# Selective scan: decays of the GpSimd steps in SBUF, exponentials and b emitted up to three steps ahead

## The chip, the core and the metric

The kernel runs on one NeuronCore of a Trainium2 chip. The core has TensorE (PE, matrix products into PSUM), VectorE (DVE), ScalarE (ACT, activation functions), GpSimd (POOL) and a queue engine SyncE (SP) that issues transfers. Each engine takes its instructions in the order in which they were put in its queue; semaphores make one engine wait for another. The metric is the device time in microseconds (us) of one execution. The kernel before takes 29,334.67 us, the median of three runs (29,313.72 to 29,365.72).

## The reference

Sixteen images of 48 x 48 positions and 96 channels go through two layers. Each layer normalises, projects to 192 channels, applies a 3 x 3 depthwise convolution and SiLU, and then runs a selective scan in four directions (row-wise and column-wise, forward and backward). After the scan come a gate, an output projection and a feed-forward block in rounded number formats; layer 0 also has a convolutional branch. Nearly all of the time goes to the scan. Cut to what matters, for each channel d, state n (16 of them) and direction:

```python
h = h * exp(delta_t * A[d, n]) + (delta_t * u_t) * B_t[n]
y_t = sum over n of h[d, n] * C_t[n]      # then + D * u_t
```

It runs over L = 2304 positions. The factor exp(delta A) is the decay; the second term is called b below.

## The kernel before, in words

**Tiles.** A scan works on tiles of 128 partitions by CH = 768 positions, in float32. The 128 partitions hold 32 channels times 4 states. One image and layer needs two passes ("pair" 0 forward, 1 backward), each over NCH = 3 chunks of 768 positions, 3 groups j of 128 channels, 4 blocks i of 32 channels, and GROUPS = 4 groups g of states: STEPS = 288 steps. There are 32 scans (16 images, 2 layers), so 9216 steps.

**One step.** In `scan`, a step n makes, in this order of the program:

1. `loaded` (L461) asks for `d` (delta and delta x u of 32 channels, repeated for 4 states; 4 buffers) when g is 0, and for `bc` (B and C of 4 states, repeated for 32 channels; 6 buffers) when these change. Both are issued on SyncE.
2. `begun` (L481) calls it, then makes the decay `a` with an exponential on ScalarE (L484) into PSUM, in one of two buffers of the pool `ps`, and the product `b` on GpSimd (L486) into one of four SBUF buffers.
3. The recurrence itself is one scan instruction on VectorE (L518): h = a h + b along 768 positions, started from the `carry` column of the chunk before.
4. The product `hc` = h x C (L520; 4 buffers).
5. ScalarE copies the last column of h into `carry` (L522).
6. TensorE multiplies `hc` with the 0/1 matrix `fold_sb` (L524) and adds it up in `py`, over the 16 steps of one j; then ScalarE copies `py` out (L533). The first addend of `py` is the skip term or the y of the forward pass, loaded as `first` (L502) and added at L504.

**Who makes hc.** `SHARE = (1, 0, 0, 0)` and the line

```python
here = SHARE[self.turn % len(SHARE)] == 0
```

split the steps. Of each four, one (g = 0) has its product made by GpSimd. [...]there the scan writes h to an SBUF tile `h` (two buffers). In the other three the scan overwrites the decay in PSUM and VectorE makes the product from there.

**Order.** Before step n's scan, the program has written down the exponential and b of step n + 1 (`ready` holds them). The program's order is not yet that of the queues: the framework's scheduler places each engine's instructions from that order and from the buffers that it expects to be free.

**Other work.** `together` runs the scan of one image beside the remaining work of its neighbours (`first`, `middle`, `final`: normalisation, convolutions, projections, gate, feed-forward). That work is a generator which is advanced in proportion to the steps done, so a given part of it always stands beside the same steps. It uses its own buffers, and all five engines.

Of the kernel before, what the change touches and what calls it, by code (L numbers as in the profile page):

```python
# [11 lines left out]
F32 = mybir.dt.float32  # L12
# [3 lines left out]
AF = mybir.ActivationFunctionType  # L16
ALU = mybir.AluOpType
# [13 lines left out]
CH = 2 * SUB  # L31
# [5 lines left out]
SHARE = (1, 0, 0, 0)  # L37
# [82 lines left out]
def sub(ap):  # L120
    return ap.rearrange("p (q f) -> p q f", f=SUB)
# [16 lines left out]
class Net:  # L138
    def __init__(self, ctx, tc, wpack, at, b2, ffw):
        self.tc, self.nc = tc, tc.nc  # L140
        nc = self.nc
# [31 lines left out]
        for t in ("l0", "l1"):  # L173
            a = self.const.tile([128, 2 * 12 * GROUPS], F32, name=t + "_a")
# [3 lines left out]
            d = self.small.tile([128, 3], F32, name="dsum")  # L178
# [8 lines left out]
        for t, bias in (("bn1", "e1b"), ("bn2", "e2b")):  # L187
# [4 lines left out]
            b = self.const.tile([128, 3], F32, name=t + "_b")  # L192
# [7 lines left out]
        for v, name in (("g", "ong"), ("b", "onb")):  # L200
            for i, half in enumerate("ab"):
                n = (128, 64)[i]
# [25 lines left out]
        for name, w, at in (  # L228
# [11 lines left out]
            d = self.dram.tile([128, 9 * 128], F32, name="taps_" + name)  # L240
# [5 lines left out]
        for i in range(2):  # L246
            d = lambda name, shape: self.dram.tile(shape, F32, name=f"{name}_{i}")
# [7 lines left out]
                    "dd": {(p, j): d(f"dd{p}{j}", [128, NCH * 2 * CH]) for p in range(2) for j in range(3)},  # L255
                }
            )
        self.turn = 0

    def get(self, name):  # L260
        at, width, rows = self.at[name]
# [186 lines left out]
    def scan(self, t, s):  # L448

        nc = self.nc  # L450
        rates = self.a[t].rearrange("p (a b i g) -> p a b i g", a=2, b=3, i=4)
        steps = []
        for pair in range(2):
            for c in range(NCH) if pair == 0 else reversed(range(NCH)):
                for j in range(3):
                    for i in range(4):
                        for g in range(GROUPS):
                            steps.append((pair, c, j, i, g))
        held = {}

        def loaded(pair, c, j, i, g):  # L461

            if g == 0:
                d = self.sw.tile([128, 2, CH], F32, name="d", bufs=4)
                rows = s["dd"][pair, j][32 * i : 32 * i + 32, c * 2 * CH : (c + 1) * 2 * CH]
                nc.sync.dma_start(
                    d.rearrange("p w f -> p (w f)"), rows.unsqueeze(1).broadcast_to([ND, NG, 2 * CH])
                )
                held["d"] = d
            kk = KK[j][32 * i]  # L470
            if (j, i) in ((0, 0), (1, 2)):
                b = self.sw.tile([128, 2, CH], F32, name="bc", bufs=6)
                at = (2 * pair + kk) * NS + g * NG
                rows = s["bc"][at : at + NG, c * 2 * CH : (c + 1) * 2 * CH]
                nc.sync.dma_start(
                    b.rearrange("p w f -> p (w f)"), rows.unsqueeze(0).broadcast_to([ND, NG, 2 * CH])
                )
                held["bc", g] = b
            return held["d"], held["bc", g]

        def begun(pair, c, j, i, g):  # L481
            d, bc = loaded(pair, c, j, i, g)
            a = self.ps.tile([128, 2, 512], F32, name="a", tag="ps").rearrange("p q f -> p (q f)")[:, :CH]
            nc.scalar.activation(a, d[:, 0, :], AF.Exp, scale=rates[:, pair, j, i, g : g + 1])  # L484
            b = self.sw.tile([128, CH], F32, name="b", bufs=4)
            nc.gpsimd.tensor_tensor(b, d[:, 1, :], bc[:, 0, :], ALU.mult)  # L486
            return a, b, bc[:, 1, :]

        ready = [begun(*steps[0])]
        before = carry = py = None  # L490
        for n, (pair, c, j, i, g) in enumerate(steps):
            if n + 1 < len(steps):
                ready.append(begun(*steps[n + 1]))
            a, b, cc = ready.pop(0)
            cs = slice(c * CH, (c + 1) * CH)
            if (j, i, g) == (0, 0, 0):
                before = carry if c != (0, NCH - 1)[pair] else None
                carry = self.sw.tile([128, 12 * GROUPS], F32, name="carry")
            if (i, g) == (0, 0):
                py = self.psy.tile([128, 2, 512], F32, name="py")  # L500
                first = self.sw.tile([128, CH], F32, name="first", bufs=1)
                nc.sync.dma_start(first, s["u" if pair == 0 else "y"][j][:, cs])  # L502
                for q in range(2):
                    nc.tensor.matmul(  # L504
                        py[:, q, :SUB],
                        lhsT=self.skip[t][:, j, :] if pair == 0 else self.ident,
                        rhs=first[:, q * SUB : (q + 1) * SUB],
                        start=True,
                        stop=False,
                    )  # L510
            way = (lambda ap: ap) if pair == 0 else (lambda ap: ap[:, ::-1])
            last = CH - 1 if pair == 0 else 0
            at = (4 * j + i) * GROUPS + g
            start = 0.0 if before is None else before[:, at : at + 1]
            here = SHARE[self.turn % len(SHARE)] == 0
            self.turn += 1
            h = a if here else self.sw.tile([128, CH], F32, name="h")
            nc.vector.tensor_tensor_scan(way(h), way(a), way(b), start, ALU.mult, ALU.add)  # L518
            hc = self.sw.tile([128, CH], F32, name="hc", bufs=4)
            (nc.vector if here else nc.gpsimd).tensor_tensor(hc, h, cc, ALU.mult)  # L520
            if c != (NCH - 1, 0)[pair]:
                nc.scalar.copy(carry[:, at : at + 1], h[:, last : last + 1])  # L522
            for q in range(2):
                nc.tensor.matmul(  # L524
                    py[:, q, :SUB],
                    lhsT=self.fold[:, i, :],
                    rhs=hc[:, q * SUB : (q + 1) * SUB],
                    start=False,
                    stop=((i, g) == (3, GROUPS - 1)),
                )  # L530
            if (i, g) == (3, GROUPS - 1):
                yt = self.sw.tile([128, CH], F32, name="yt", bufs=1)
                nc.scalar.copy(sub(yt), py[:, :, :SUB])  # L533
                nc.scalar.dma_start(s["y"][j][:, cs], yt)
            yield
# [245 lines left out]
def together(scan, others):  # L781


    total = sum(WORK[name] for name, _ in others)

    def all_others():
        for _, gen in others:
            yield from gen

    other, done = all_others(), 0  # L790
    for n, _ in enumerate(scan):
        while done < total * (n + 1) / (AHEAD * STEPS):
            done += next(other, 1e9)
    for _ in other:
        pass


@with_exitstack
def metaformer_kernel(ctx: ExitStack, tc: tile.TileContext, x, wpack, at, b2, ffw, fold, out):

    nc = tc.nc
    net = Net(ctx, tc, wpack, at, b2, ffw)
    net.fold = net.const.tile([128, 4, 128], F32, name="fold_sb")
    nc.scalar.dma_start(net.fold.rearrange("p a b -> p (a b)"), fold)
    image = lambda ap, m: ap[m].rearrange("(s p) c -> p s c", p=128)
    first = lambda m: ("first", net.first(m % 2, image(x, m)))
    middle = lambda m: ("middle", net.middle(m % 2, image(x, m)))
    final = lambda m: ("final", net.final(m % 2, image(out, m)))
    scan = lambda t, m: net.scan(t, net.s[m % 2])

    for _ in first(0)[1]:
        pass
    for m in range(0, NB, 2):
        together(scan("l0", m), [final(m - 1), first(m + 1)] if m else [first(m + 1)])
        together(scan("l0", m + 1), [middle(m)])
        together(scan("l1", m), [middle(m + 1)])
        together(scan("l1", m + 1), [final(m), first(m + 2)] if m + 2 < NB else [final(m)])
    for _ in final(NB - 1)[1]:
        pass
# [83 lines left out]
```

## Time and profile before

| What | Value |
|---|---|
| median of three runs | 29,334.67 us |
| the profiled execution | 29,326.56 us |
| its span, first to last instruction | 29,324.8 us |
| mean granted TensorE clock | 0.898 |
| busy: PE / VectorE / ScalarE / GpSimd | 82% / 80% / 48% / 79% |
| transfers | 4,406 MB, 150 GB/s, transfer engines 42% busy |

The profile describes one execution. Each group of instructions has its line, engine and operation, the tiles written and read (out<-in) with their shapes, the count, the total busy time, the mean duration in ns, and the idle time of the engine just before the instructions with what ended it ("<-"). A line of the view of waits reads: engine and tile that waited, "<-", what it waited for; then us in total, how many times, and the longest. Busy PE time is modelled from the ends of matmuls. The view by stretches gives the busy time of each engine in a stretch of the span, with the number of instructions in brackets, and behind them the TensorE clock, the busy share of the transfer engines and GB/s.

### The profile page before, as it was taken

What the parts mean: (1) busy time and instruction counts of PE and PEld (TensorE: products, weight loads), DVE (VectorE), ACT (ScalarE), POOL (GpSimd) and SP (SyncE); (2) the same over time, 40 slices, a digit from 0 to 9 for tenths busy, and PEclk for the clock granted to TensorE, in tenths of its full rate; (3) what the DMA queues carried; (4) which work ended last, traced back from release to release, by engine and by line L of the source; (5) the groups of instructions that cost most, each with busy time, mean ns of one, the idle gap of its engine ahead of it and who ended that gap; (6) DMA issues with size and microseconds to landing.
All of it is one profiled execution on the core that took longest, in us unless ns stands there. A gap on an engine that the chain in (4) does not pass through costs nothing. (4 is left out here: it accounts for less than half of the span.)

```text
span 29324.8 us, 227106 instructions
## 1 busy us (share of the span) xinstructions
PE 24033.6 (82%) x68224; PEld 12726.8 (43%) x68224; DVE 23488.3 (80%) x18372; ACT 14074.7 (48%) x22093; POOL 23241.6 (79%) x13238
## 2 busy tenths in 40 slices
PE   7888878888788887888788887888778888788886
PEld 3444444444444444444444444444444444344443
DVE  6877888778887788877888778887788877888777
ACT  4454444544445454444444444444444444444443
POOL 6877788778887788877888778787787877877777
PEclk8988899989999899998999989999898998989988
DMA  4444444444444444444444444444444344443443
GB/s 155 153 156 152 146 148 155 154 151 149 148 152 154 154 152 148 148 156 149 159 143 151 151 149 160 144 148 153 150 164 145 141 154 150 162 148 143 150 156 109
DMA packets 1062581, 4406.37 MB, mean 150 GB/s; under 512 B 211936, under 2 KB 211936, under 8 KB 1030368
## 3 DMA queue, kind: packets, MB, share of 16 engines
q1 hardware_dynamic: 869792, 3757.78, 36.2%
q10 hardware_dynamic: 191552, 634.06, 5.5%
q8 instruction: 536, 8.78, 0.1%
q14 instruction: 701, 5.74, 0.1%
HBM read 3500.22 MB, written 891.22 MB: 150 GB/s over the span
## 5 line engine op out<-in xcount | busy, mean ns | idle before, releaser
L486 POOL TENSOR_TENSOR b<-d,bc 128x768 f32<-128x768 f32 x9216 | 16584.7, 1819 | 4084.2 <-DVE a L518 2783.7
L524 PE MATMUL py<-hc,fold_sb 128*128 128x384 f32 x36864 | 14564.0, 540 | 3265.9 <-DVE hc L520 1991.2
L524 PEld LDWEIGHTS py<-hc,fold_sb 128*128 128x128 f32 x36864 | 7359.8, 208 | 9807.3 <-DVE hc L520 3050.8
L484 ACT ACTIVATE a<-d,l_a 128x768 f32<-128x768 f32 x9216 | 8304.2, 906 | 5248.7 <-DVE h L518 2817.0
L518 DVE TENSOR_TENSOR_SCAN a<-a,carry,b 128x768 f32<-128x768 f32 x4608 | 8252.7, 1813 | 2037.9 <-ACT a L484 1438.6
L520 DVE TENSOR_TENSOR hc<-a,bc 128x768 f32<-128x768 f32 x6912 | 6427.8, 947 | 1034.1 <-PE py L524 873.5
L520 POOL TENSOR_TENSOR hc<-h,bc 128x768 f32<-128x768 f32 x2304 | 4187.6, 1818 | 1511.8 <-DVE h L518 1115.4
L518 DVE TENSOR_TENSOR_SCAN a<-a,b 128x768 f32<-128x768 f32 x2304 | 4002.9, 1755 | 1091.6 <-ACT a L484 612.1
L522 ACT COPY carry<-a 128x1 f32<-128x1 f32 x4608 | 725.2, 158 | 5229.7 <-DVE hc L520 5210.7
L518 DVE TENSOR_TENSOR_SCAN h<-a,carry,b 128x768 f32<-128x768 f32 x1536 | 2766.9, 1801 | 484.0 <-ACT a L484 354.4
L333 PE MATMUL pst<-e,dg 128*128 128x384 f32 x5184 | 1730.3, 486 | 0.0
L430 PE MATMUL pst<-dts,wpack_sb 24*128 24x384 f32 x2304 | 1200.8, 636 | 513.9 <-ACT dl L431 434.2
L518 DVE TENSOR_TENSOR_SCAN h<-a,b 128x768 f32<-128x768 f32 x768 | 1337.2, 1741 | 303.9 <-POOL b L486 236.0
L333 PEld LDWEIGHTS pst<-e,dg 128*128 128x128 f32 x5184 | 977.2, 189 | 705.5 <-PE py L524 25.5
L333 PE MATMUL pst<-wxa,dg 128*128 128x384 f32 x3456 | 1173.3, 492 | 24.9 <-DMA dg<-taps_l0a 20.0
L442 POOL TENSOR_TENSOR du<-dl,u 128x768 f32<-128x768 f32 x576 | 1033.6, 1809 | 201.2 <-DMA dd<-du 100.4
L333 PE MATMUL pst<-wxb,dg 128*128 128x384 f32 x3456 | 1169.7, 489 | 5.6 <-issue 5.6
L431 ACT ACTIVATE dl<-pst,wpack_sb 128x384 f32<-128x384 f32 x1152 | 644.0, 577 | 1072.5 <-PE pst L430 581.4
L430 PEld LDWEIGHTS pst<-dts,wpack_sb 24*128 24x128 f32 x2304 | 446.7, 223 | 1206.6 <-ACT dl L431 661.4
L504 PE MATMUL py<-first,ident 128*128 128x384 f32 x1152 | 570.7, 629 | 484.5 <-ACT yt L533 479.6
L412 PE MATMUL pst<-u,wpack_sb 128*24 128x384 f32 (+1 forms) x2304 | 831.7, 492 | 65.2 <-ACT u L395 23.0
L333 PEld LDWEIGHTS pst<-wxa,dg 128*128 128x128 f32 x3456 | 661.5, 192 | 509.4 <-issue 44.6
(143 smaller groups left out, 15283.5 us busy)
## 6 DMA issues: line engine op xcount, KB each, us to landing
d<-dd SPq DMA_DIRECT2D x2304, 768.0 KB, 4.6
bc<-bc SPq DMA_DIRECT2D x1536, 768.0 KB, 6.0
dd<-dl ACTq DMA_DIRECT2D x192, 1152.0 KB, 4.7
dd<-du SPq DMA_DIRECT2D x576, 384.0 KB, 2.5
y<-yt ACTq DMA_DIRECT2D x576, 384.0 KB, 3.1
u<-u ACTq DMA_DIRECT2D x96, 1152.0 KB, 5.1
first<-u SPq DMA_DIRECT2D x288, 384.0 KB, 3.3
first<-y SPq DMA_DIRECT2D x288, 384.0 KB, 3.1
```

Of the source, the lines that this page charges most:

```text
L333: nc.tensor.matmul(img(o[:, :SUB]), lhsT=dg[:, k, :], rhs=img(p, PW)[:, PQ * q + i : PQ * q + i + PQ, j : j + HW], start=(k == 0), stop=(k ...
L412: nc.tensor.matmul(o[:m, :SUB], lhsT=w[:, j, :], rhs=u[j][:, cs], start=(j == 0), stop=(j == 2))
L430: nc.tensor.matmul(o[:, :SUB], lhsT=dtw[:, col, :], rhs=dts[:, cs], start=True, stop=True)
L431: nc.scalar.activation(dl[:, cs], o[:, :SUB], AF.Identity, bias=self.get(t + "dtb")[:, col : col + 1])
L442: nc.gpsimd.tensor_tensor(du, dl[:, cs], u[j][:, cs], ALU.mult)
L484: nc.scalar.activation(a, d[:, 0, :], AF.Exp, scale=rates[:, pair, j, i, g : g + 1])
L486: nc.gpsimd.tensor_tensor(b, d[:, 1, :], bc[:, 0, :], ALU.mult)
L504: nc.tensor.matmul(py[:, q, :SUB], lhsT=self.skip[t][:, j, :] if pair == 0 else self.ident, rhs=first[:, q * SUB : (q + 1) * SUB], start=True,
L518: nc.vector.tensor_tensor_scan(way(h), way(a), way(b), start, ALU.mult, ALU.add)
L520: (nc.vector if here else nc.gpsimd).tensor_tensor(hc, h, cc, ALU.mult)
L522: nc.scalar.copy(carry[:, at : at + 1], h[:, last : last + 1])
L524: nc.tensor.matmul(py[:, q, :SUB], lhsT=self.fold[:, i, :], rhs=hc[:, q * SUB : (q + 1) * SUB], start=False, stop=((i, g) == (3, GROUPS - 1)),
```

## The change

The tiles of the exponentials are chosen by who makes the product, and the emission of exponentials and b is separated from the step.

- `decay(n)` makes the exponential. For a step whose product VectorE makes, the decay is in PSUM as before. For a step whose product GpSimd makes, it goes to the SBUF tile `h` (two buffers, as before).
- The scan always works in place: from `a` and `b` into `a`. For GpSimd's steps both of its inputs are now in SBUF.
- `added(n)` makes b on GpSimd, `loads_of(n)` asks for `d` and `bc`.
- `begin(n + 3, psums)` runs after each step's scan, product and carry copy, and ahead of its matmuls. It emits b up to step n + 3. It emits exponentials up to step n + 3 too, but stops at a PSUM step when two earlier PSUM decays have not yet been used (`psums` counts those that have). Before, one step was emitted ahead, before the scan.

Pools and their buffer counts, the number of instructions and transfers, and everything outside `scan` stay as they were.

```diff
-        def begun(pair, c, j, i, g):
-            d, bc = loaded(pair, c, j, i, g)
-            a = self.ps.tile([128, 2, 512], F32, name="a", tag="ps").rearrange("p q f -> p (q f)")[:, :CH]
-            nc.scalar.activation(a, d[:, 0, :], AF.Exp, scale=rates[:, pair, j, i, g : g + 1])
-            b = self.sw.tile([128, CH], F32, name="b", bufs=4)
-            nc.gpsimd.tensor_tensor(b, d[:, 1, :], bc[:, 0, :], ALU.mult)
-            return a, b, bc[:, 1, :]
-
-        ready = [begun(*steps[0])]
+        loads, decays, inputs = {}, {}, {}
+
+        def loads_of(n):
+            if n not in loads:
+                loads[n] = loaded(*steps[n])
+            return loads[n]
+
+        def decay(n):
+
+            pair, c, j, i, g = steps[n]
+            if here(n):
+                a = self.ps.tile([128, 2, 512], F32, name="a", tag="ps").rearrange("p q f -> p (q f)")[:, :CH]
+            else:
+                a = self.sw.tile([128, CH], F32, name="h")
+            nc.scalar.activation(a, loads_of(n)[0][:, 0, :], AF.Exp, scale=rates[:, pair, j, i, g : g + 1])
+            decays[n] = a
+
+        def added(n):
+            d, bc = loads_of(n)
+            inputs[n] = self.sw.tile([128, CH], F32, name="b", bufs=4)
+            nc.gpsimd.tensor_tensor(inputs[n], d[:, 1, :], bc[:, 0, :], ALU.mult)
+
+        def here(n):
+            return SHARE[n % len(SHARE)] == 0
+
+        begun, psums = [0, 0], 0
+
+        def begin(n, psums):
+
+            while begun[0] <= min(n, len(steps) - 1):
+                k = begun[0]
+                if here(k):
+                    if sum(map(here, range(k))) >= psums + 2:
+                        break
+                decay(k)
+                begun[0] += 1
+            while begun[1] <= min(n, len(steps) - 1):
+                added(begun[1])
+                begun[1] += 1
+
+        begin(2, 0)
         before = carry = py = None
         for n, (pair, c, j, i, g) in enumerate(steps):
-            if n + 1 < len(steps):
-                ready.append(begun(*steps[n + 1]))
-            a, b, cc = ready.pop(0)
+            a, b, cc = decays.pop(n), inputs.pop(n), loads.pop(n)[1][:, 1, :]
...
-            here = SHARE[self.turn % len(SHARE)] == 0
-            self.turn += 1
-            h = a if here else self.sw.tile([128, CH], F32, name="h")
-            nc.vector.tensor_tensor_scan(way(h), way(a), way(b), start, ALU.mult, ALU.add)
+            nc.vector.tensor_tensor_scan(way(a), way(a), way(b), start, ALU.mult, ALU.add)
             hc = self.sw.tile([128, CH], F32, name="hc", bufs=4)
-            (nc.vector if here else nc.gpsimd).tensor_tensor(hc, h, cc, ALU.mult)
+            (nc.vector if here(n) else nc.gpsimd).tensor_tensor(hc, a, cc, ALU.mult)
             if c != (NCH - 1, 0)[pair]:
-                nc.scalar.copy(carry[:, at : at + 1], h[:, last : last + 1])
+                nc.scalar.copy(carry[:, at : at + 1], a[:, last : last + 1])
+            if here(n):
+                psums += 1
+            begin(n + 3, psums)
```

More of the change, by code (lines that the diff above doesn't have):

```diff
@@ L257, in __init__ @@
             )
-        self.turn = 0
     def get(self, name):
```

## The prediction

> **What bounds the kernel now.** I read the page first: busy shares, then the costliest groups.
>
> ```profile
> PE 24033.6 (82%) x68224; PEld 12726.8 (43%) x68224; DVE 23488.3 (80%) x18372; ACT 14074.7 (48%) x22093; POOL 23241.6 (79%) x13238
> L486 POOL TENSOR_TENSOR b<-d,bc 128x768 f32<-128x768 f32 x9216 | 16584.7, 1819 | 4084.2 <-DVE a L518 2783.7
> L518 DVE TENSOR_TENSOR_SCAN a<-a,carry,b 128x768 f32<-128x768 f32 x4608 | 8252.7, 1813 | 2037.9 <-ACT a L484 1438.6
> L518 DVE TENSOR_TENSOR_SCAN h<-a,carry,b 128x768 f32<-128x768 f32 x1536 | 2766.9, 1801 | 484.0 <-ACT a L484 354.4
> L520 DVE TENSOR_TENSOR hc<-a,bc 128x768 f32<-128x768 f32 x6912 | 6427.8, 947 | 1034.1 <-PE py L524 873.5
> L520 POOL TENSOR_TENSOR hc<-h,bc 128x768 f32<-128x768 f32 x2304 | 4187.6, 1818 | 1511.8 <-DVE h L518 1115.4
> ```
>
> No engine is full over the whole span: PE, VectorE and GpSimd share the load at about 80% each. Call the 2304 steps whose product GpSimd makes N, and the other 6912 H. Four steps, one N and three H, are a cycle. There are 2304, so one takes 29,324.8 / 2304 = 12.73 us. A cycle holds 4 x 1.80 + 3 x 0.95 = 10.05 us of scans and products on VectorE, and 5 x 1.82 = 9.1 us on GpSimd (4 b, 1 product). All work added, VectorE has 10.19 and GpSimd 10.09 us a cycle. So some 2.5 us a cycle are waiting. The view of waits says for what:
>
> ```profile
> ACT a L484 <- DVE h L518: 2817.0, 1267, 9.1
> POOL b L486 <- DVE a L518: 2783.7, 1504, 16.6
> ACT a L484 <- DVE hc L520: 2277.3, 961, 5.9
> DVE a L518 <- ACT a L484: 2050.8, 1411, 13.0
> ```
>
> ScalarE waits for VectorE to let go of a decay, and VectorE then waits for ScalarE: the ping-pong of two PSUM buffers. The exponential takes 0.906 us, so where nothing lies between a release and the next scan VectorE idles about 1.1 us. The scans waited for the exponentials for 2050.8 us and, with the h scans, 2,412.7 us in all; for carry copies another 1,035.
>
> That is the average. The kernel mixes other work into the scan, so I cut one period (two images, four scans, 3660 us from 11,000 us on) into 61 stretches of 60 us. Columns: stretch, length, then PE, weight load, VectorE, ScalarE, GpSimd busy.
>
> ```profile
> 11000.00:11060.00 60.00, 39.64 (x87) 19.43 (x88) 51.98 (x38) 24.98 (x27) 59.03 (x32) 0.83 0.48 176
> 11240.00:11300.00 60.00, 45.70 (x157) 26.89 (x157) 59.41 (x52) 24.83 (x49) 52.44 (x30) 0.98 0.37 132
> 12140.00:12200.00 60.00, 60.00 (x184) 33.61 (x182) 50.50 (x41) 27.14 (x50) 45.33 (x26) 1.00 0.42 154
> 12440.00:12500.00 60.00, 51.13 (x158) 28.60 (x157) 47.13 (x36) 30.85 (x58) 48.75 (x30) 0.94 0.48 161
> 12500.00:12560.00 60.00, 46.37 (x136) 26.48 (x135) 38.76 (x29) 31.16 (x43) 37.63 (x24) 0.89 0.42 150
> ```
>
> These are four regimes. In 5 stretches GpSimd is full (first row), in 7 VectorE (second), in 7 PE (third). The rest have no full engine (fourth and fifth rows), and only there can shorter waits buy time.
>
> [...]The kernel before always reads the decay, or h in place of it, from PSUM, so its scans never have two SBUF inputs and this trace does not show the case. It does show the lock with the conversions[...]:
>
> ```profile
> L722 DVE TENSOR_SCALAR h<-h,l_b x576: 284/771/1956, 1461.6 to 29314.7; 128x384 f16<-128x384 f16 x192
> ```
>
> The line gives minimum, median and maximum: an instruction of 284 ns takes up to 1956, that is, it waits for up to 1.67 us, about one GpSimd instruction and no more; on average (878 ns in the view of groups) 0.59.
>
> [...]
>
> **The change part by part.** Counts stay: 9216 exponentials, b, scans and products each; 2304 d loads and 1536 bc loads.
>
> 1. *N decays in SBUF.* Removed: one of four claims on the two PSUM buffers, so the exponential for an H step no longer waits for an N scan. Ceiling of the gain: the 2,412.7 us of VectorE's waits for exponentials, or 1.05 us a cycle; most lie where no engine is full. ScalarE's cost: 2304 writes to SBUF; I allow 0 to 50 ns, at most 115 us on an engine 48% busy, so hidden by its idle time. If that cover were gone, it would be 115 us.
>
> 2. *The N scan reads two SBUF operands.* [...]I take 1.80, no gain. The lock: each N scan and GpSimd's instructions exclude each other, and all of GpSimd's large ones read SBUF. So GpSimd's time and N scans add: 23,241.6 + 2304 x 1.80 = 27,389 us, 11.89 a cycle. VectorE also waits for the instruction under way: 0.6 us (the measured mean of L722) to 1.8 (it arrives just as b ends and GpSimd goes on): 1,382 to 4,147 us.[...] Queued behind a blocked N scan are the H scans and their products, which PE and the carries wait for; behind a blocked GpSimd instruction are the next b, which VectorE waits for.
>
> 3. *The order.* The framework's scheduler lays out the queues. Compiled, all 9216 scans stood in step order before; now an N scan stands one place earlier in 363 cases, two in 1327, three in 332. On GpSimd the product of an N step stood most often (1497 of 2304) behind the b of three steps later, now most often (1051) of four. The b still has four buffers, so its real lead is not longer. I charge nothing for order itself; GpSimd's time hides it, and the ACT rival prices the failure.
>
> 4. *Exponentials and loads ahead.* The N exponential now stands ahead of three to five H exponentials on ScalarE. It waits for a buffer h (two of them) that GpSimd's product two N steps back releases; the H exponentials and carry copies queue behind it, and VectorE waits for those. The loads on SP are asked for up to three steps ahead, past the loads of "first" and du's stores; d and bc keep 4 and 6 buffers, and SP waits mostly for those to be released, so they land when they did. GpSimd's 815.6 us waits for bc may shrink: gain 0 to 815 us; I take 0 since the buffers decide.
>
> *The sum*, by stretch. For each I take the largest of: PE busy; GpSimd busy + 1.80 x N scans; VectorE busy + 0.6 x N scans. N scans are a quarter of the scans in the stretch (22 in the first row: 59.03 + 5.5 x 1.80 = 68.9; 23 in the second: 52.44 + 10.35 = 62.8; 20 in the fourth: 57.8; 16 in the fifth: PE's 46.4). In 26 stretches the result exceeds 60 us and adds up to 1,655 in place of 1,560; in 35 it stays below and adds up to 1,951 in place of 2,100. The first are losses that cannot be avoided; I add 2% for two handovers of about 0.12 us in a cycle of 11.9: 1,688. Of the 149 us in the second I take half, since table loads, PE and carries keep part of the waits: 2,025. Together 3,713 for 3,660, or +1.45%. 29,324.8 x 1.0145 = 29,750 us of span. The profiled execution took 29,326.6, 1.8 more than its span, and the median 29,334.7 is 8 above that: 29,760 us, some 425 more than before.
>
> **Rivals.**
>
> *Released waits outweigh the lock* (faster). All 149 us are had and the losses stay at 1,655: 3,606, -1.5%, 28,890 us. The place is the stretches without a full engine; it decides where 86% of the 149 us are had (128 are lost with the handovers), or 64% without handovers. For it: scans' waits for ACT are VectorE's largest. Against it: 20 of the 26 losing stretches lose on GpSimd's bound, which no buffer eases.
>
> *No lock for scans*[...]. The bound falls to 3,358 of 3,660. The kernel now reaches 92% of its own; at 96%: 3,498, -4.4%, 28,030 us. For it: the trace has no such scan. Against it: [...]L722.
>
> *ScalarE blocked behind GpSimd* (much slower). Take the order scan N, product, H scan, product, product, H scan, with the N exponential ahead of the second H exponential. N scan 1.8, then b, b, product on GpSimd 5.4, N exponential 1.1, carry and H exponential 1.1, H scan 1.8, the next H scan 1.8: 13.0 us, with 0.14 of VectorE's other work 13.14, +3.2%: 30,280 us, and more where GpSimd's other work (1.0 us a cycle) falls into the chain. It decides where two or more b stand between the locked scan and that product. Against it: in the commonest order only the product itself does, and GpSimd's sum of 11.9 covers it.
>
> **How the numbers follow.** Chances: forecast (0.2 to 3% slower) 0.56; ScalarE blocked (3% and beyond) 0.11; waits outweigh 0.19; no lock 0.08; within 0.2% 0.06. About 0.2% is what a measurement of this kernel can tell from no change. So faster 0.27, same 0.06, slower 0.67. The range goes from the waits' case, 28,800, to just past the blocked case, 30,600; the no-lock case and worse ones are left out, near 2 in 10. The forecast's own range is 29,400 to 30,250.
>
> **What would show it.** Right: GpSimd's mean for b and product rises from 1.82 by up to 4147 / 11,520 = 0.36 us, and the N scan's from 1.80 to between 2.4 and 3.6; waits of exponentials for h scans (2817.0) vanish; PE-full stretches keep their length, GpSimd-full ones grow by some 15%. The N scan at 1.74 to 1.80 with b at 1.82 means no lock. Long waits of the exponentials for GpSimd's product mean the blocked queue. If both groups stretch and the time still falls, the waits were worth more than half of what I gave them.

## The result and the profile after

The changed kernel takes 32,419.0 us, the median of four runs (32,404.2 to 32,424.0). The kernel before took 29,347.6 beside it. The ratio is 1.1047, with a 95% interval from 1.1033 to 1.1061: 10.5% slower, and above the range that was forecast.

The page of the changed kernel, parts 1 and 5. The lines answer to those shown of before; the line numbers have moved (L500 is b, L544 the scan, L546 the product, L494 the exponential).

```profile
span 32420.2 us, 222342 instructions
PE 24962.2 (77%) x68224; PEld 13034.9 (40%) x68224; DVE 25607.6 (79%) x18372; ACT 14085.8 (43%) x22093; POOL 25353.8 (78%) x13238
L500 POOL TENSOR_TENSOR b<-d,bc 128x768 f32<-128x768 f32 x9216 | 18383.7, 2012 | 5733.7 <-DVE a L544 3644.0
L544 DVE TENSOR_TENSOR_SCAN a<-a,carry,b 128x768 f32<-128x768 f32 x4608 | 8252.1, 1811 | 2402.1 <-ACT a L494 2302.1
L544 DVE TENSOR_TENSOR_SCAN h<-h,carry,b 128x768 f32<-128x768 f32 x1536 | 4042.8, 2632 | 1237.0 <-POOL b L500 1058.6
L544 DVE TENSOR_TENSOR_SCAN h<-h,b 128x768 f32<-128x768 f32 x768 | 2095.4, 2728 | 623.1 <-POOL b L500 472.2
L494 ACT ACTIVATE h<-d,l_a 128x768 f32<-128x768 f32 x2304 | 2151.7, 934 | 6355.1 <-POOL hc L546 6282.9
L546 POOL TENSOR_TENSOR hc<-h,bc 128x768 f32<-128x768 f32 x2304 | 4341.1, 1884 | 768.0 <-PE py L553 384.0
```

The same instructions are done, the same number of times, yet two groups got longer. The N scans with a carry take 2,632 ns on average in place of 1,801, those without 2,728 (before: 1,741). GpSimd's b takes 2,012 in place of 1,819. The H scans, whose decay is in PSUM, stay at 1.81 and 1.75. So the lock is there.

The view of waits after:

```profile
ACT h L494 <- POOL hc L546: 6282.9, 1841, 9.4
POOL b L500 <- DVE a L544: 3644.0, 1971, 15.6
DVE a L544 <- ACT a L494: 3443.8, 1558, 15.7
DVE h L544 <- POOL b L500: 1530.7, 823, 7.8
```

ScalarE's wait for the h scans (2,817.0 us before) is gone. In its place stands one of 6,282.9 us for GpSimd's product. VectorE waits longer for the exponentials of the H steps than before (2,050.8), which was what the change was to shorten. Its N scans now wait 1,530.7 us for b, 823 times (before: 297.3, 54 times).

A few lines of the timeline after show the lock, either way round. Columns: start, duration, engine, line and operation; in brackets the idle time ahead and what ended it.

```profile
15718.92 1.79 DVE L544 TENSOR_TENSOR_SCAN h<-h,carry,b 128x768 f32<-128x768 f32 x1
15719.09 3.22 POOL L500 TENSOR_TENSOR b<-d,bc 128x768 f32<-128x768 f32 x1 [0.30 <-DVE a L544]
...
15724.04 3.56 POOL L500 TENSOR_TENSOR b<-d,bc 128x768 f32<-128x768 f32 x2
15724.11 0.94 ACT L494 ACTIVATE h<-d,l_a 128x768 f32<-128x768 f32 x1 [1.61 <-POOL hc L546]
...
15725.88 3.34 DVE L544 TENSOR_TENSOR_SCAN h<-h,carry,b 128x768 f32<-128x768 f32 x1 [2.58 <-POOL b L500]
```

At 15,718.9 the N scan starts first and takes its plain 1.79 us; the b that comes 0.17 us later takes 3.22 us, 1.4 more than usual. At 15,725.9 it is the other way round: the scan has waited 2.58 us for its b, the first of the two that start at 15,724.0. As that ends, GpSimd goes on to the second, and the scan takes 3.34 us, until that one is through and 1.6 us more. In both cases the instruction that starts first takes its plain time, and the other is longer. It is so throughout the trace: of the 2,304 N scans, 642 begin while GpSimd does nothing, and take 1.78 us on average; 1,662 begin inside an instruction of GpSimd, and 97% of these end 1.5 to 1.9 us after that instruction. Of the 9,216 b, 1,304 begin inside an N scan and take 3.21 us on average, and 99% of these end 1.5 to 2.0 us after that scan; the 2,969 that begin inside an H scan take 1.81 us, the others 1.82.

ScalarE's blocked queue, elsewhere in the same timeline:

```profile
13407.74 1.80 POOL L546 TENSOR_TENSOR hc<-h,bc 128x768 f32<-128x768 f32 x1
...
13409.58 0.93 ACT L494 ACTIVATE h<-d,l_a 128x768 f32<-128x768 f32 x1 [6.70 <-POOL hc L546]
...
13410.59 0.90 ACT L494 ACTIVATE a<-d,l_a 128x768 f32<-128x768 f32 x1
...
13411.52 1.82 DVE L544 TENSOR_TENSOR_SCAN a<-a,carry,b 128x768 f32<-128x768 f32 x1 [4.91 <-ACT a L494]
```

The N exponential has stood 6.70 us at the head of the queue, until GpSimd's product freed a buffer h. An H exponential stands behind it, and VectorE has waited 4.91 us for that one.

The next table compares all runs, which are described below, by VectorE's busy time, which includes what a scan stands in the lock, and the rest of the span. Times of the profiled executions, in us; the last column is the ratio of the medians to the kernel before with its interval.

| kernel | span | VectorE busy | VectorE idle | GpSimd busy | ratio |
|---|---|---|---|---|---|
| before | 29,325 | 23,488 | 5,836 | 23,242 | 1 |
| after | 32,420 | 25,608 | 6,813 | 25,354 | 1.1047 (1.1033 to 1.1061) |
| h4 | 31,569 | 25,751 | 5,819 | 25,346 | 1.0759 (1.0743 to 1.0775) |
| ahead_only | 29,275 | 23,506 | 5,770 | 23,226 | 0.9967 (0.9957 to 0.9978) |
| sbuf_only | 32,393 | 25,530 | 6,863 | 25,313 | 1.1047 (1.1030 to 1.1063) |
| apart | 31,510 | 25,577 | 5,933 | 25,288 | 1.0740 (1.0724 to 1.0756) |
| lock_only | 30,481 | 24,834 | 5,647 | 24,911 | 1.0399 (1.0383 to 1.0414) |
| half | 30,703 | 24,722 | 5,980 | 24,294 | 1.0466 (1.0448 to 1.0483) |
| h4_nocarry | 31,061 | 25,626 | 5,434 | 25,268 | 1.0581 (1.0566 to 1.0597) |
| ahead_b6 | 29,682 | 23,571 | 6,111 | 23,198 | 1.0124 (1.0109 to 1.0139) |
| apart_steps | 30,261 | 24,644 | 5,617 | 25,798 | 1.0308 (1.0293 to 1.0324) |
| after_steps | 31,851 | 24,234 | 7,617 | 25,706 | 1.0851 (1.0833 to 1.0869) |

From before to after, VectorE's busy time grew by 2,119 us and its idle time by 976. These make up the 3,095 us of the span.

### The profile page after: what moved, and what is told of

The parts are those of the page before. It is cut to its first block, busy times and chain, and to the rows that moved or that the text cites. A ratio compares the mean times of both kernels' runs of the same rounds, so it can differ in the third digit from the quotient of the medians.

```text
span 32420.2 us, 222342 instructions
## 1 busy us (share of the span) xinstructions
PE 24962.2 (77%) x68224; PEld 13034.9 (40%) x68224; DVE 25607.6 (79%) x18372; ACT 14085.8 (43%) x22093; POOL 25353.8 (78%) x13238
## 5 line engine op out<-in xcount | busy, mean ns | idle before, releaser
L500 POOL TENSOR_TENSOR b<-d,bc 128x768 f32<-128x768 f32 x9216 | 18383.7, 2012 | 5733.7 <-DVE a L544 3644.0
L553 PE MATMUL py<-hc,fold_sb 128*128 128x384 f32 x36864 | 15150.1, 556 | 4282.8 <-DVE hc L546 2868.3
L553 PEld LDWEIGHTS py<-hc,fold_sb 128*128 128x128 f32 x36864 | 7551.6, 214 | 11247.0 <-DVE hc L546 4174.7
L544 DVE TENSOR_TENSOR_SCAN a<-a,carry,b 128x768 f32<-128x768 f32 x4608 | 8252.1, 1811 | 2402.1 <-ACT a L494 2302.1
L494 ACT ACTIVATE a<-d,l_a 128x768 f32<-128x768 f32 x6912 | 6201.7, 902 | 2596.1 <-DVE hc L546 2438.8
L546 DVE TENSOR_TENSOR hc<-a,bc 128x768 f32<-128x768 f32 x6912 | 6432.2, 944 | 822.3 <-PE py L553 644.3
L544 DVE TENSOR_TENSOR_SCAN h<-h,carry,b 128x768 f32<-128x768 f32 x1536 | 4042.8, 2632 | 1237.0 <-POOL b L500 1058.6
L544 DVE TENSOR_TENSOR_SCAN a<-a,b 128x768 f32<-128x768 f32 x2304 | 4012.7, 1752 | 1211.9 <-ACT a L494 1141.7
L546 POOL TENSOR_TENSOR hc<-h,bc 128x768 f32<-128x768 f32 x2304 | 4341.1, 1884 | 768.0 <-PE py L553 384.0
L494 ACT ACTIVATE h<-d,l_a 128x768 f32<-128x768 f32 x2304 | 2151.7, 934 | 6355.1 <-POOL hc L546 6282.9
L544 DVE TENSOR_TENSOR_SCAN h<-h,b 128x768 f32<-128x768 f32 x768 | 2095.4, 2728 | 623.1 <-POOL b L500 472.2
L548 ACT COPY carry<-h 128x1 f32<-128x1 f32 x1536 | 292.7, 191 | 3216.9 <-DVE h L544 3216.9
L411 PE MATMUL pst<-u,wpack_sb 128*24 128x384 f32 (+1 forms) x2304 | 909.5, 529 | 255.6 <-ACT u L394 130.3
```

The costliest lines, as they stand in the source:

```text
L411: nc.tensor.matmul(o[:m, :SUB], lhsT=w[:, j, :], rhs=u[j][:, cs], start=(j == 0), stop=(j == 2))
L494: nc.scalar.activation(a, loads_of(n)[0][:, 0, :], AF.Exp, scale=rates[:, pair, j, i, g : g + 1])
L500: nc.gpsimd.tensor_tensor(inputs[n], d[:, 1, :], bc[:, 0, :], ALU.mult)
L544: nc.vector.tensor_tensor_scan(way(a), way(a), way(b), start, ALU.mult, ALU.add)
L546: (nc.vector if here(n) else nc.gpsimd).tensor_tensor(hc, a, cc, ALU.mult)
L548: nc.scalar.copy(carry[:, at : at + 1], a[:, last : last + 1])
```

## The experiments

Three theories were set against each other. The queue theory: the loss comes from ScalarE's queue, which stands behind GpSimd's product. The lock theory: it comes from N scans and GpSimd excluding each other. The order theory: emitting exponentials and b ahead is itself what costs.

**Which half of the change costs.** First the order alone, with the decays in PSUM:

```diff
-            if here(n):
-                a = self.ps.tile(...)
-            else:
-                a = self.sw.tile([128, CH], F32, name="h")
+            a = self.ps.tile(...)
...
-                if here(k):
-                    if sum(map(here, range(k))) >= psums + 2:
-                        break
+                if k >= psums + 2:
+                    break
...
-            nc.vector.tensor_tensor_scan(way(a), way(a), way(b), start, ALU.mult, ALU.add)
+            h = a if here(n) else self.sw.tile([128, CH], F32, name="h")
+            nc.vector.tensor_tensor_scan(way(h), way(a), way(b), start, ALU.mult, ALU.add)
```

> Only the order part: exponentials and b are emitted up to three steps ahead as in the changed kernel, but every decay is in PSUM (two buffers) and the N scan writes to h, as before. No N scan has two SBUF inputs, and no exponential needs an h. Queue and lock theories: both costs are gone, so 28,800 to 29,700 us, about the kernel before. Order theory (moving b and exponentials ahead itself upsets the queues): 31,000 us or more.

Measured: 29,245.1 us. Then the place alone: the kernel before, with N decays in SBUF scanned in place.

```diff
+            if SHARE[g] == 0:
                 a = self.ps.tile(...)
+            else:
+                a = self.sw.tile([128, CH], F32, name="h")
...
-            h = a if here else self.sw.tile([128, CH], F32, name="h")
+            h = a
```

> Only the place part: N decays in SBUF, scanned in place, two buffers h, but one step emitted ahead and before the scan, as in the kernel before. Lock theory: the lock is whole, so 31,500 to 32,500 us. Queue theory: the exponential still takes its h from GpSimd's product, so 31,000 to 32,500 too if the scheduler puts it equally early; ScalarE's wait for that product then is again above 4,000 us. Order theory: 29,300 to 30,000.

Measured: 32,421.4 us, the changed kernel's time to within 0.1%. So the whole loss comes from the decays in SBUF, however far ahead the program writes things down; emission three steps ahead alone gains 0.33%, and this version is faster than both kernels. The theory that the emission order itself upsets the queues fell. The profile of this run has the queue's wait too:

```profile
ACT h L487 <- POOL hc L523: 6110.8, 1794, 10.8
```

**ScalarE's queue.** Four buffers h in place of two:

```diff
-                a = self.sw.tile([128, CH], F32, name="h")
+                a = self.sw.tile([128, CH], F32, name="h", bufs=4)
```

> The changed kernel with four buffers h in place of two, nothing else. Queue theory (the N exponential stands at the head of ScalarE's queue and waits for GpSimd's product to free h, which it did for 6,282.9 us): with four buffers it needs the product of four N steps back, long done; that wait falls below 1,500 us and the time by at least 1,500, to 29,600 to 30,900 us. Lock theory (what costs is that N scans and GpSimd exclude each other): the lock is untouched, so the time stays within 400 us of 32,420, and the N scan's mean stays above 2.6 us.

And the N decay in tiles of its own, scanned into h:

```diff
-                a = self.sw.tile([128, CH], F32, name="h")
+                a = self.sw.tile([128, CH], F32, name="an")
...
-            nc.vector.tensor_tensor_scan(way(a), way(a), way(b), start, ALU.mult, ALU.add)
+            h = a if here(n) else self.sw.tile([128, CH], F32, name="h")
+            nc.vector.tensor_tensor_scan(way(h), way(a), way(b), start, ALU.mult, ALU.add)
```

> The changed kernel, but the N decay has SBUF tiles of its own (two) and the scan writes to h (two), so it is not in place: the exponential then waits for the N scan two N steps back on VectorE, not for GpSimd's product, and the scan for h. The lock is untouched. Queue theory: ScalarE's wait for GpSimd's product vanishes, 29,600 to 30,900 us, like four buffers. Lock theory: within 400 us of 32,420.

Measured: 31,574.5 and 31,514.0 us. Both theories missed: 845 and 905 us came back where the queue theory wanted 1,500 and the lock theory none. The waits behaved as the queue theory said. In neither run does a wait of ScalarE for GpSimd's product stand among the long ones, and VectorE's idle time falls by 994 and 880 us, back to that of the kernel before. What stays is 2,000 us and more of VectorE's busy time, that is, the lock.

**The lock by itself.** In the kernel before, the N scan gets a second SBUF input and nothing is moved:

```diff
-            nc.vector.tensor_tensor_scan(way(h), way(a), way(b), start, ALU.mult, ALU.add)
+            if here:
+                nc.vector.tensor_tensor_scan(way(h), way(a), way(b), start, ALU.mult, ALU.add)
+            else:
+                nc.vector.tensor_tensor_scan(way(h), way(self.flat), way(b), a[:, 0:1], ALU.mult, ALU.add)
```

> The kernel before, with the lock alone added: an N scan reads a constant SBUF tile (0.5 everywhere) in place of its decay, and takes one column of the PSUM decay as its start value, so that it waits for the same exponential and frees the same PSUM buffer. The recurrence of the N steps is left out by this (their decays and carried starts aren't used). The compiled orders are the ones of before but for a few cycles. Lock theory: the 7.4% that stay with four buffers are the lock; the N scan's mean rises from 1.8 to about 2.6 us, GpSimd's b from 1.82 to about 2.0, and the time to 31,200 to 31,700 us. Rival, that the moved orders and the earlier N exponentials make most of it: below 30,400 us.

Measured: 30,505.2 us, +4.0%. Its profile:

```profile
L523 DVE TENSOR_TENSOR_SCAN h<-flat,a,b 128x768 f32<-128x768 f32 x2304 | 5420.1, 2352 | 839.0 <-POOL b L488 374.7
L488 POOL TENSOR_TENSOR b<-d,bc 128x768 f32<-128x768 f32 x9216 | 18005.5, 1974 | 3426.6 <-DVE a L521 2029.5
```

The order is that of before, so these 1,160 us are the lock alone: a second SBUF input stretches the scan by 0.57 us on average (2,352 against (1536 x 1,801 + 768 x 1,741) / 2304 = 1,781 ns) and b by 0.16. But the lock theory had wanted all of what four buffers and separate decays leave (7.6% and 7.4%). It fell in that form, as the other theory did (below 30,400). Something makes the same lock dearer in the changed kernel: there the N scan stands 0.88 us in it.

Half as many locked scans, in the version with separate decays:

```diff
+        def placed(n):
+            return here(n) or n // 4 % 2 == 0
...
-            if here(n):
+            if placed(n):
                 a = self.ps.tile(...)
```

(and `placed` in place of `here` where the PSUM decays are counted.)

> The version with separate SBUF decays, but for every second N step only; the other N steps have their decay in PSUM as before. 1152 locked scans in place of 2304. Lock theory: the surcharge over the order-only version (29,245) is proportional, half of 2,270: 30,200 to 30,600 us. Rival, that a few locked scans already upset the queues or that only the last ones hurt: outside 29,900 to 30,900.

Measured: 30,699.9 us. The surcharge over the order alone is 1,455 us, 64% of the 2,269 with all N steps. That lies between the two ranges, so both theories missed: the cost is not quite proportional. The scans in the lock take longer than with all N steps (2,753 and 3,006 ns against 2,632 and 2,835), and those with PSUM decays stay at 1.80 and 1.74.

**Where the N scan stands.** In the changed kernel the scheduler put it one to three places early, 2,022 times of 2,304. It did so in the run with the place alone too (2,005), and never in the run with the order alone: the early scan comes with the decay in SBUF and not with the emission ahead. Pinned to step order, as before, in the version with separate decays and in the changed kernel:

```diff
-            nc.vector.tensor_tensor_scan(way(a), way(a), way(b), start, ALU.mult, ALU.add)
+            h = a if here(n) else self.sw.tile([128, CH], F32, name="h")
+            with self.tc.issue_after(pinned) if pinned is not None else nullcontext():
+                scanned = nc.vector.tensor_tensor_scan(way(h), way(a), way(b), start, ALU.mult, ALU.add)
+            pinned = scanned.ins
```

(This is the version with separate decays; in the changed kernel the scan stays in place.)

> The version with separate SBUF decays, with the scans pinned to step order on VectorE (as they stand in the kernel before); nothing else is pinned. The lock is whole; ScalarE needs no product of GpSimd. Early-scan theory (the N scan, moved up to three places ahead, stands on VectorE waiting for its own b, and meets GpSimd just as it goes on to the next b): waits of N scans for b fall from 1,936 below 800 us, the N scan's mean from 2.7 towards the 2.35 us of the lock alone, and the time to 30,400 to 30,900 us. Rival, that the lock costs 7.4% wherever the scan stands and the lock alone looked cheap only because the exponentials' waits hid it: 31,200 to 31,600 us.

> The changed kernel with the scans pinned to step order on VectorE, two buffers h as in it. Queue theory: the N exponential still waits for GpSimd's product to free h, so some 850 us more than with separate decays in the same order. Early-scan theory: 900 to 1,000 us off the changed kernel's 32,419, 31,400 to 31,700. Rival: unchanged, 32,200 to 32,500.

Measured: 30,257.6 and 31,846.3 us. The first lies even below the range that was given to it, the second above its own. Compare the N scans with a carry in the version with separate decays, first early, then in step order. The numbers are minimum, median and maximum in ns.

```profile
L545 DVE TENSOR_TENSOR_SCAN h<-an,carry,b x1536: 1780/2575/7312, 383.8 to 31320.4; 128x768 f32<-128x768 f32 x192
```

```profile
L546 DVE TENSOR_TENSOR_SCAN h<-an,carry,b x1536: 1784/1819/6907, 380.0 to 30071.6; 128x768 f32<-128x768 f32 x192
```

In step order the median scan is hardly held (1,819), and more often it is GpSimd that stands: its b takes 2,070 ns in that run, 1,997 with early scans. Early, the median loses 0.8 us. The reason is in the timeline above: a scan that waits for the b just being made starts when GpSimd has already begun the next instruction, and so stands until that one is through (3.34 us in that line). In the changed kernel the 823 scans that waited for b take 3.03 us on average, the others 2.46. This also answers why the same lock is dearer there than by itself: about as many scans begin inside an instruction of GpSimd (1,662 against 1,620), but on average 1.36 us of it are still to come in place of 0.87. In step order its b has been ready for a while, and the waits of N scans for b fall from 1,936 to 450 us:

```profile
L546 DVE TENSOR_TENSOR_SCAN h<-an,carry,b 128x768 f32<-128x768 f32 x1536 | 3418.4, 2226 | 236.9 <-POOL b L500 126.5 <-ACT an L494 110.4
L546 DVE TENSOR_TENSOR_SCAN h<-an,b 128x768 f32<-128x768 f32 x768 | 1773.0, 2309 | 323.3 <-POOL b L500 323.3
```

Of the 1,249 us between the two spans, 933 are VectorE's busy time. GpSimd takes over part of it: it is 510 us busier.

The changed kernel in step order shows the queue bare. It was expected to differ from the separate decays in step order by some 850 us; it differs by 1,589, and the gain was 573 where 900 to 1,000 were expected. VectorE is less held (24,234 us busy) but idles for 7,617, since ScalarE waits even longer:

```profile
ACT h L494 <- POOL hc L548: 7243.1, 1901, 10.8
DVE a L545 <- ACT a L494: 3024.3, 1266, 13.6
DVE a L545 <- ACT carry L550: 2059.1, 945, 14.0
```

So the two costs overlap: early scans cost 573 us where the queue holds and 1,256 where it doesn't; the queue costs 905 with early scans and 1,589 without.

**Carry copies.** With four buffers, ScalarE waited 4,102.8 us for the N scan ahead of its carry copy.

```diff
-            start = 0.0 if before is None else before[:, at : at + 1]
+            start = 0.0 if before is None or not here(n) else before[:, at : at + 1]
...
-            if c != (NCH - 1, 0)[pair]:
+            if c != (NCH - 1, 0)[pair] and here(n):
```

> Four buffers h, and the N steps start from zero and copy no carry (the carried state of the N steps is left out): 1536 copies less on ScalarE, which with four buffers waited 4,102.8 us for the N scan at the head of its queue. Lock theory: this wait is off the path; the time stays within 250 us of 31,574. Rival, ScalarE's queue still holds the H exponentials back behind the N scan: 31,000 us or less.

Measured: 31,037.7 us, 537 less, just short of the rival's bracket and outside the lock theory's. This wait was on the path, in part: VectorE idles 385 us less, and is 124 us less busy.

**A longer lead for b.** The order alone, with six buffers b (`bufs=6` in `added`).

> The order part alone, with six buffers b in place of four, so that being emitted three steps ahead also means a longer lead on GpSimd. No lock. If GpSimd's waits for a free b (2,786.9 us) were on the path: 28,500 to 29,050 us. If only the exchange of the two PSUM buffers between ScalarE and VectorE bounds it: 29,150 to 29,350.

Measured: 29,702.1 us, slower than with four by 457 us, outside both brackets. GpSimd's waits for VectorE fall (2,786.9 to 2,203.5 us), but those for bc more than double:

```profile
L497 POOL TENSOR_TENSOR b<-d,bc 128x768 f32<-128x768 f32 x9216 | 16537.9, 1818 | 4421.8 <-DVE a L541 2203.5 <-DMA bc<-bc 1924.7 <-DVE h L541 217.3
```

The queues are laid out anew when a buffer count changes. Whether bc's six buffers or the order of the loads keeps the data back, no run tells.

## Why the prediction was wrong

**The lock held, in its sizes too.** An N scan of 2.63 to 2.73 us lies in the 2.4 to 3.6 that were given; b grew by 0.19 us where up to 0.36 were allowed. That a scan with two SBUF inputs would be held at all was an assumption that the trace before did not show. The rival without a lock is out.

**Which terms failed.** A path through the runs adds up to the whole: the order alone 29,245 us (ahead_only); the lock with the scans in step order 1,012 more (apart_steps); the scans early 1,256 more (apart); ScalarE's queue behind GpSimd's product 905 more, which makes the changed kernel's 32,419. The prediction's 425 were, per period of 3,660 us, a loss of 128 for the lock (1,688 for 1,560), which is about 1,025 over the span, less 75 for half of the waits, about 600. So the lock's term had the right size. Wrong were "I charge nothing for order itself", which measured 1,256 us; the blocked queue, which is not in the sum and measured 905; and the credit of 600. Taken the other way round, the last two steps of the path are 1,589 for the queue and 573 for the early scans.

The stretches in which the sum was made show where. The table has the same steps in each run, matched by the count of H scans, in us. The 26 stretches are those in which the sum exceeds 60 us; the 7 with PE full had PE busy for 58 us or more, and their column is the mean of one.

| | 26 stretches | 35 stretches | all 61 | 7 with PE full |
|---|---|---|---|---|
| before | 1,560 | 2,100 | 3,660 | 60.0 |
| the prediction | 1,688 | 2,025 | 3,713 | 60 |
| ahead_only | 1,568 | 2,086 | 3,654 | 60.0 |
| lock_only | 1,664 | 2,140 | 3,804 | 60.1 |
| apart_steps | 1,695 | 2,077 | 3,772 | 60.4 |
| h4 | 1,733 | 2,200 | 3,933 | 62.1 |
| apart | 1,729 | 2,203 | 3,932 | 62.8 |
| after | 1,778 | 2,275 | 4,053 | 72.2 |

With the scans in step order the 26 losing stretches come out as forecast, 1,695 for 1,688, and the others lose nothing (40 with the lock by itself): there most of the lock sinks into waits. Early scans cost most in these others (126 of 160 us). The stretches with PE full were to keep their length. They do so with the lock alone; in the changed kernel they grow by a fifth, and four buffers h bring them back to 62.1. So it is ScalarE's queue that lengthens them.

**Released waits: no gain.** Of the 75 us credited per period, the 35 stretches gained 23 in step order, 14 of which the order alone has too; in the changed kernel they lost 175. Even with four buffers and no wait for GpSimd, H scans wait 2,364.1 us for exponentials; after, 3,443.8. The waits for the h scans vanished as said, and others took their place. The rival in which they outweigh the lock is out.

**Time in the lock.** I took 0.6 us per N scan, the mean of the short conversions (427 of the 576 begin inside an instruction of GpSimd in the trace before, and 411 of these end 0.11 to 0.21 us after it), and gave 1.8 for a scan that arrives as b ends. The runs show both as cases of one thing: 0.57 us with the scan where it stood and 0.88 with it early, of which those that waited for b lose 1.25 and the others 0.68.

**"I charge nothing for order itself"** failed by the scan and not by the emission. The compiled order, which the prediction read, showed the scan up to three places early with only four buffers b; that its b would then often come last and fresh was there to be seen.

**ScalarE behind GpSimd's product** was described rightly (step 4 and the third rival) and thought unlikely, since GpSimd's sum would cover it. Its wait of 6,282.9 us is the longest of all. At 905 us (with early scans) to 1,589 (in step order) its price is 3% to 5%, near the 3.2% that the rival gave, but it had been put in place of the lock's cost and not on top of it. A cycle now takes 32,420.2 / 2304 = 14.07 us: 12.73 before, 0.92 of VectorE's longer busy time, 0.42 of longer idle time.

**Small terms held.** The exponentials into SBUF take 934 ns in the changed kernel against 902 into PSUM, 32 ns more and within the 50, which were an allowance of mine. The scan out of SBUF was charged no gain, and shows none: the 432 N scans with a carry that begin in the changed kernel while GpSimd does nothing take 1,802 ns on average, those with a carry before 1,801. GpSimd's waits for bc did not shrink (815.6 to 967.9).

What remains open: the 1,012 us hold the lock's price and whatever the freed PSUM claims gave, and no run parts the two; the lock by itself, with nothing freed, costs 1,160. And pinning the scans moved other queues along. GpSimd's product stands behind the b of four steps later in 1,061 cases with early scans, in step order behind that of three steps later in 1,314. So the 1,256 us are the scan's place together with this.

## What to carry to other kernels

Here a buffer's place also decided whether a scan and GpSimd hold each other up: the scan took 1.74 to 1.81 us with its decay in PSUM, 2.63 to 2.73 with both inputs in SBUF. Before an operand of VectorE moves from PSUM to SBUF beside a busy GpSimd, price the lock (here 0.57 us per scan where the scan stood, 0.88 where it came early) and ask what else the new place moves. Here the lock itself was a third of the loss; the place also let the scheduler put the scan early, and tied the exponential to GpSimd. A tile that is written earlier than before is held earlier too, so ask whose slow consumer frees it and what stands behind the writer in its queue. And let the instruction that can be held start when its input has been ready for a while: here, putting the scans back in step order shifted part of the cost to the other engine and took 1,256 us off.

## What was not expected of the hardware

The lock's cost moves between the engines with the order: the extra busy time is 2,119 us on VectorE and 2,112 on GpSimd in the changed kernel, 1,156 and 2,556 with separate decays and scans in step order. The sum is not fixed: it goes from 3,016 us with the lock alone to 4,367 with four buffers h.

The granted TensorE clock fell from 0.898 to 0.865 in the slower kernel, in which PE was busy for 77% of the span in place of 82%; the same fold matmuls took 556 ns in place of 540, and PE's busy time rose from 24,034 to 24,962 us. In the step-order version with separate decays it is 0.877, in the order alone 0.895. No run separates this from the changed order on PE. The waits don't show it slowing the kernel: VectorE's products wait less for PE than before (644.3 us against 873.5).
